# Three bf16 feature terms, 16-bit weights and running counts in PSUM in the ranked pass of a four-layer graph network

## The chip, the cores and the metric

The kernel runs on one core of a Trainium2 chip. The metric is device time in microseconds (us), the median over several executions. The engines of a core are named as the profile names them: PE (TensorE, matrix products; PEld is its weight load), DVE (VectorE), ACT (ScalarE), POOL (GpSimd) and SP (SyncE, which here issues the loads of the large matrix). PE multiplies from SBUF into PSUM, the accumulator memory, which the kernel uses in units of one bank: 128 partitions by 512 f32 values. The other engines read sums from there.

## The reference

Four layers on a graph of N = 3327 nodes with D = 64 features and a dense 3327 x 3327 f32 matrix `adj` (about half a per cent of its entries are not zero). Each layer normalizes x, applies a relu, and adds a graph network's result to x:

```python
# layer 0: two gated cells, each with m = adj @ (x @ W)
gi = m @ wih.T + bih;  gh = x @ whh.T + bhh
r = sigmoid(i_r + h_r);  z = sigmoid(i_z + h_z)
n = tanh(i_n + r * h_n)
x = relu((1.0 - z) * n + z * x)

# layer 1: ranked weights
support = input @ weight
mask = (adj != 0)
rank = cumsum(mask, axis=1);  deg = rank[:, -1:]
k = minimum(deg, 100.0)
pos = rank - (deg - k)
w = mask * where(pos > 0, 0.5 ** (k - pos), 0.0)
out = w @ support + bias

# layer 2: w = adj * adj; three times x = (w @ x) @ W.T + b
# layer 3: two times x = tanh(concat([adj @ x, x]) @ W[k])
```

That is eight passes over the matrix: two with adj, one with the ranked weights of layer 1, three with the squares, two with adj again. In the ranked weights an entry that is not zero counts the entries of its row that lie behind it, n of them, and weighs 0.5 to the power n if n is below 100.

## The kernel before

**Layout.** The nodes are padded to 26 blocks of 128, in two halves `s` of 13 blocks. The features of both halves stand side by side, so that a product with 128 weight columns comes as two instructions of 64 (`for h in range(2)`), one for each half. The nodes are cut into four chunks `CH` of 3, 3, 3 and 4 blocks: a chunk's sum is 384, 384, 384 or 512 columns wide. Chunks 0 and 1 are group 0, chunks 2 and 3 group 1 (`GROUPS`).

**Tiles of the matrix.** A tile is one block row of `adjT` (a source block `q`, 128 partitions) by the columns of one group in both halves, 768 or 896 KB. SP loads it into one of 19 slots `adj0` to `adj18` (L248). 286 loads are made. The list `units` holds the whole work in order as (pass, chunk, tile). `alone(g, k, order, sweep)` puts one pass for one group, tile by tile with both chunks of each, but for the last `sweep` tiles, which all go through chunk a first and then through chunk b, so that chunk a's sum is complete early. `joint` lets a tile serve two passes. The stages in order are: pass 0 of group 0, passes 0 and 1 of group 1, pass 1 of group 0, then pass 2 (the ranked pass) of group 0 and of group 1 with the source blocks in descending order and `sweep=0`, pass 3 of group 1, and four more (L584 to L594).

**One unit.** `run()` (L392) goes through the units. It prepares tiles 8 or 16 units ahead (`prepare`: load, and in the ranked pass the mask, L286, and the running count, L291), expands two units ahead (`expand`) and multiplies (`propagate`, L335): the chunk's sum in PSUM gains y of the source block times the tile's columns. On PE the ranked pass thus reads: counts of unit i+2, product of unit i, counts of unit i+3, and so on.

**Ranked weights.** `expand` counts in PSUM for each entry the entries behind it. The bf16 matrix `tri` counts inside a block (and subtracts 128 on the diagonal, which tells where the entry itself is not zero); `ones` times the running count of the blocks behind (`before.after`) adds the rest. Both go into a tile `ps` with two banks, one for each half s. L316 then makes 0.5 to the power n from that count on ACT: it scales by -2^23, adds a bias, clips at zero and writes the result as an int32 whose bits are read as an f32. The running count is the sum over all blocks before (L291, on DVE), in bf16, and lies with the mask in one slot (`Counts`). The product L335 takes y in f32, and 2^27 is worked into it beforehand (L452).

**PSUM.** Eight banks are drawn from two pools: four tiles `acc` of one bank each for the chunks' sums, and two tiles `ps` of two banks each, which all other products use (L310 in `expand`, `temps()` and `temp()` elsewhere).

**After a sum.** When a chunk has met its 26 source blocks, `propagate` starts that chunk's task, a generator `after_k`. It first copies the sum to SBUF (`evacuate`, L410 on DVE for even chunks, L408 on ACT for odd ones), then makes dense products and the normalization. `spend()` takes the time of each unit (`STREAM_US`) off every task's remaining delay and lets the task go on when that is used up, so the `yield` values set at which place among the products a task's instructions stand. `gru` (L465) makes the gated cell of layer 0: products for r and z into one tile `prz`, for n into another tile `pn` (L470), two sigmoids (L478, L479), two operations that read `pn` (L483, L484), tanh and the rest. `residual` (L457) adds to x from PSUM. `add_row` (L462, POOL) adds a bias. `after_1` normalizes with the factor 2^27 for the ranked pass and ends with `y[2][c] = yk`; the product of the ranked pass that needs this y finishes that task first.

The order of the instructions on every engine is the order in which this program emits them; nothing is moved later.

Of the kernel before, what the change touches and what calls it, by code (L numbers as in the profile page):

```python
# [11 lines left out]
I32 = mybir.dt.int32  # L12
# [26 lines left out]
N, D = 3327, 64  # L39
# [11 lines left out]
TWO23 = float(2 ** 23)  # L51
# [29 lines left out]
def kernel(  # L81
# [14 lines left out]
    psum = ctx.enter_context(tc.tile_pool(name="psum", bufs=4, space=bass.MemoryType.PSUM))  # L96
# [25 lines left out]
    ones = const.tile([P, P], BF16, name="ones")  # L122
# [4 lines left out]
    def more_constants():  # L127
        for h in range(2):
            hs = slice(h * D, (h + 1) * D)
            nc.vector.tensor_copy(bd[hs, :, hs], packed[hs])  # L130
        nc.gpsimd.memset(ones, 1.0)

        nc.gpsimd.affine_select(out=tri, in_=ones, pattern=[[-1, P]], compare_op=ALU.is_gt, fill=0.0,
                                base=0, channel_multiplier=1)
        nc.gpsimd.affine_select(out=tri, in_=tri, pattern=[[-1, P]], compare_op=ALU.not_equal, fill=-128.0,
                                base=0, channel_multiplier=1)
        nc.gpsimd.memset(bitsb, (CAP - 128.0) * TWO23)
        wide = work.tile([P, P], F32, name="t2")
        nc.gpsimd.memset(wide, 0.0)

        for i, (bi, bh) in enumerate(((BI1, BH1), (BI2, BH2))):
            nc.vector.tensor_add(bsum[:, i], bcol[:, bi:bi + 2], bcol[:, bh:bh + 2])

        nc.vector.tensor_scalar(wide[0:D], wide[0:D], bcol[0:D, BL1:BL1 + 1], None, op0=ALU.add)
        yield 3.0
        ps = temp()
        mm(ps[:, :D], wide, ident[:, :D])
        nc.vector.tensor_copy(brow[:, 3], ps[:, :D])

        for wt, ih in ((W1, IH1), (W2, IH2)):  # L150
            yield 1.0
            ps = temp()
            mm(ps[:, :P], bd[:, wt, :], ident)
            tr = work.tile([P, P], F32, name="t2")
            nc.scalar.copy(tr, ps[:, :P])
            yield 1.0
            ps = temp()
            mm(ps[:, :3 * P], tr, bd[:, ih:ih + 3, :].rearrange("p g f -> p (g f)"))
            nc.vector.tensor_copy(bd[:, ih:ih + 3, :].rearrange("p g f -> p (g f)"), ps[:, :3 * P])

# [4 lines left out]
    def width(c):  # L165
        return blocks(c) * P

    def mm(out, lhsT, rhs, start=True, stop=True):


        for h in range(2):
            hs = slice(h * D, (h + 1) * D)
            nc.tensor.matmul(out[hs], lhsT[:, hs], rhs, start=start, stop=stop)  # L173

    def temps():
        return psum.tile([P, 2, CWM], F32, name="ps", bufs=2)

    def temp():
        return temps()[:, 0]
# [21 lines left out]
    tasks = {}  # L201

    def advance(c):
        try:
            tasks[c][1] = next(tasks[c][0])
        except StopIteration:
            del tasks[c]

# [9 lines left out]
    def spend(us):  # L218

        for c in list(tasks):  # L220
            tasks[c][1] -= us
            if tasks[c][1] <= 0:
                advance(c)
# [8 lines left out]
    class Tile:  # L232

        def __init__(self, q, g, in_place):
            self.q, self.g, self.in_place, self.uses = q, g, in_place, 0
            self.b0 = CH[GROUPS[g][0]][0]
            self.w = sum(width(c) for c in GROUPS[g])
            self.slot = self.counts = self.before = None
            self.squares = set()
# [20 lines left out]
    class Counts:  # L260


        def __init__(self, w):
            self.slot = dead.popleft()
            both = slots[self.slot].bitcast(BF16).rearrange("p s w -> p (s w)")
            self.mask, self.after = (
                both[:, i * 2 * GWM:i * 2 * GWM + 2 * w].rearrange("p (s w) -> p s w", s=2) for i in range(2))

        def free(self):
            dead.append(self.slot)  # L270
# [9 lines left out]
    def prepare(k, c, t):  # L280

        if t.slot is None:
            t.load()
        if KIND[k] == RANKED and t.counts is None:
            t.counts, t.before = Counts(t.w), newest.get(t.g)
            nc.vector.tensor_scalar(t.counts.mask, t.view(), 0.0, None, op0=ALU.not_equal)  # L286
            t.used()
            if t.before is None:
                t.counts.after = t.counts.mask
            elif t.q > 0:  # L290
                nc.vector.tensor_tensor(t.counts.after, t.before.after, t.counts.mask, ALU.add)  # L291
            newest[t.g] = t.counts
        if KIND[k] == SQUARED and t.in_place and c not in t.squares:
            t.squares.add(c)
            square(t.view(c), t.view(c), t.q + c)

    def expand(k, c, t):

        w = width(c)
        if KIND[k] == PLAIN or t.in_place:  # L300
            return t.view(c)
        wide = work.tile([P, 2, CWM], F32, name="w4", bufs=4)[:, :, :w]
        if KIND[k] == SQUARED:
            square(wide, t.view(c), t.q + c)
            return wide

        ps = temps()  # L310
        for s in range(2):
            mm(ps[:, s, :w], tri, t.counts.mask[:, s, t.cols(c)], stop=t.before is None)
            if t.before is not None:
                mm(ps[:, s, :w], ones, t.before.after[:, s, t.cols(c)], start=False)
        spend(STREAM_US * w / CWM)
        nc.scalar.activation(wide.bitcast(I32), ps[:, :, :w], AF.Relu, bias=bitsb, scale=-TWO23)  # L316
        if c == GROUPS[t.g][1]:
            if t.before is not None:
                t.before.free()
            if t.q == 0:  # L320
                t.counts.free()
        return wide

    def propagate(k, c, t, rhs, first, last):
        w = width(c)
        s, b = divmod(t.q, NB)
        cs = chunk_of(b)
        if y[k][cs] is None:
            finish(cs)
        if first:  # L330
            sums[k, c] = psum.tile([P, CWM], F32, name="acc")
        acc = sums[k, c]
        yq = y[k][cs][:, b - CH[cs][0], s, :]
        for h in range(2):
            nc.tensor.matmul(acc[h * D:(h + 1) * D, :w], yq, rhs[:, h, :], start=first, stop=last)  # L335
        if KIND[k] != RANKED:
            t.used()
        spend(STREAM_US * w / CWM)
        if last:
            begin(c, after[k](c, sums.pop((k, c))))  # L340

# [63 lines left out]
    def evacuate(acc, c):  # L405
        m = work.tile([P, CWM], F32, name="t2")[:, :width(c)]
        if c % 2:
            nc.scalar.copy(m, acc[:, :width(c)])  # L408
        else:
            nc.vector.tensor_copy(m, acc[:, :width(c)])  # L410
        return m

    def dense_to_nodes(terms, c):

        v = view(temp(), c)
# [4 lines left out]
        return v  # L420

    def transpose_to_nodes(ft, c):
        v = view(temp(), c)
        for b in range(blocks(c)):
            mm(v[:, b, :], ft[:, b * P:(b + 1) * P], ident)
        return v

    def transpose_to_features(h, c):
        ps = temp()
# [3 lines left out]
        nc.scalar.copy(ft, ps[:, :width(c)])  # L433
        return ft
# [21 lines left out]
    def residual(v, c):  # L456
        nc.vector.tensor_tensor(flat(xchunk(c)), flat(xchunk(c)), v, ALU.add)  # L457
# [7 lines left out]
    def gru(acc, c, hT, ih, hh, bi, bh, cell):  # L465
# [4 lines left out]
        prz, pn = temps(), temps()  # L470
        for g in range(2):
            mm(prz[:, g, :w], bd[:, hh + g, :], hT, stop=False)
            mm(prz[:, g, :w], bd[:, ih + g, :], m, start=False)
        for g, (wt, ft) in enumerate(((hh + 2, hT), (ih + 2, m))):
            mm(pn[:, g, :w], bd[:, wt, :], ft)
        rz = work.tile([P, 2, CWM], F32, name="w4", bufs=4)
        r, z = rz[:, 0, :w], rz[:, 1, :w]
        nc.scalar.activation(r, prz[:, 0, :w], AF.Sigmoid, bias=bsum[:, cell, 0:1])  # L478
        nc.scalar.activation(z, prz[:, 1, :w], AF.Sigmoid, bias=bsum[:, cell, 1:2])  # L479
# [3 lines left out]
        nc.vector.scalar_tensor_tensor(t, pn[:, 0, :w], bcol[:, bh + 2:bh + 3], r, op0=ALU.add, op1=ALU.mult)  # L483
        nc.vector.tensor_tensor(t, t, pn[:, 1, :w], ALU.add)  # L484
# [8 lines left out]
        return o  # L493

# [9 lines left out]
    def after_0(c, acc):  # L504
        hT[c] = yield from gru(acc, c, hT[c], IH1, HH1, BI1, BH1, 0)
        v = transpose_to_nodes(hT[c], c)
        yield 0.8
        yk = nodes(c)
        nc.vector.tensor_copy(flat(yk), v)
        y[1][c] = yk  # L510

    def after_1(c, acc):
# [7 lines left out]
        y[2][c] = yk  # L520
# [12 lines left out]
    def after_hop(k):  # L533
        def done(c, acc):
# [6 lines left out]
            nc.vector.tensor_tensor(groups(yk), v.rearrange("p b (s d) -> p (b s) d", d=D),  # L541
                                    brow[:, k - 3:k - 2, :].to_broadcast([P, n, D]), ALU.add)
            y[k + 1][c] = yk
# [14 lines left out]
    def after_6(c, acc):  # L558
# [4 lines left out]
        nc.scalar.activation(flat(yk), v, AF.Tanh)  # L563
# [4 lines left out]
    def after_7(c, acc):  # L568
# [4 lines left out]
        nc.scalar.activation(flat(t), v, AF.Tanh)  # L573
        yield 0.8
        residual(flat(t), c)
# [68 lines left out]
```

## Time and profile before

The profile is of one execution; its time lies 0.55 us above the median of the runs.

| | us |
|---|---|
| median of 9 runs (lowest, highest) | 769.35 (768.61, 769.9) |
| the profiled execution's own time | 769.9 |
| its span in the profile | 766.9 |
| ranked products, sum of 104 units (L335 from `w`, with the squares not made in place) | 128.2 busy |
| ranked counts (L173, `tri` and `ones`) | 72.9 + 70.8 busy |
| running counts on DVE (L291), 48 times | 50.6 busy |
| masks on DVE (L286), 52 times | 53.8 busy |
| weights on ACT (L316), 104 times | 99.3 busy |

A row of a group reads: line, engine, operation, output from inputs, shape and type, how often; then busy time and the mean in ns of one; then the idle time of the engine just before these instructions, and what ended most of it. Consecutive matmuls overlap in the records, so a matmul's own duration is longer than the step from one start to the next. A row of a timeline reads: start, duration, engine, line, operation, output from inputs, shape, number; in brackets the engine's idle time before it and what ended it. The idle time before the copies L410 is DVE's, not PE's.

### The profile page before, as it was taken

The page shows a single profiled execution, that of the slowest core. Times are in us where ns is not written, and L with a number is a line of the kernel's source. Part 1 is how long each engine was busy: PE and PEld are TensorE (multiplying, and loading weights), DVE is VectorE, ACT ScalarE, POOL GpSimd, SP SyncE. Part 2 cuts the span into 40 slices and gives each one's busy share as a digit, 9 for nine tenths or more (in the row PEclk, how much of TensorE's full clock was granted, in tenths as well). Part 3 has the DMA queues.
Part 4 walks back from the last instruction along what each step waited for, and adds up shares of the span by engine and source line. Part 5 has one row for each costly group of instructions (what it writes and reads, how often), then busy time and mean ns, then how long its engine had stood idle before and what let it go on. Part 6 is the DMA issues. An engine that isn't in the chain of part 4 may idle for free.

```text
span 766.9 us, 11891 instructions
## 1 busy us (share of the span) xinstructions
PE 735.0 (96%) x5032; PEld 349.4 (46%) x5032; DVE 278.4 (36%) x386; ACT 247.1 (32%) x306; POOL 44.4 (6%) x37
## 2 busy tenths in 40 slices
PE   3978999999989999999999999999999999999997
PEld 2423433444545555556434444434344445344444
DVE  6102101226779958970774121513062520000000
ACT  1101001011046676666985431733034601000000
POOL 5000000002003001200200000000020010000000
PEclk9999999999999999999999999999999999999999
DMA  9999994789977998999999948990998389915991
GB/s 290 401 401 406 406 406 172 274 320 403 401 268 253 331 355 290 314 359 406 406 402 400 401 191 320 405 404 15 352 391 294 136 304 405 379 59 196 401 402 73
DMA packets 79172, 245.25 MB, mean 320 GB/s; under 512 B 4880, under 2 KB 5520, under 8 KB 79120
## 3 DMA queue, kind: packets, MB, share of 16 engines
q1 hardware_dynamic: 78240, 243.55, 84.5%
q10 hardware_dynamic: 880, 0.96, 0.5%
q8 instruction: 39, 0.64, 0.3%
q14 instruction: 13, 0.11, 0.0%
HBM read 243.64 MB, written 0.85 MB: 319 GB/s over the span
## 4 chain that ended last, share of the span: by engine, by line
PE 83%; DMA 8%; DVE 6%; SPq 1%; ACT 1%; issue 1%; POOL 0%; ACTq 0%; DVEq 0%; POOLq 0%
PE acc L335 67%; PE ps L173 16%; DMA adj<-in_adjT 7%; SPq L248 1%; DMA brow<-in_bias_rows 1%; DVE adj L291 1%; DVE adj L286 1%; ACT w L316 1%; DVE xs L457 0%; DVE st L447 0%; DVE st L441 0%; DVE w L276 0%; DVE t L446 0%; DVE t L443 0%; DVE w L483 0%
## 5 line engine op out<-in xcount | busy, mean ns | idle before, releaser
L335 PE MATMUL acc<-adj,y 128*64 128x384 f32 (+1 forms) x2704 | 489.6, 516 | 20.9 <-DMA adj<-in_adjT 20.5
L335 PEld LDWEIGHTS acc<-adj,y 128*64 128x64 f32 x2704 | 194.3, 137 | 286.4 <-issue 235.0
L335 PE MATMUL acc<-w,y 128*64 128x384 f32 (+1 forms) x624 | 128.2, 504 | 1.7 <-DVE w L276 0.8
L410 DVE COPY t<-acc 128x384 f32<-128x384 f32 x16 | 8.9, 558 | 294.4 <-PE acc L335 294.4
L316 ACT ACTIVATE w<-ps,bitsb 128x768 int32<-128x768 f32 x104 | 99.3, 956 | 48.8 <-PE ps L173 45.6
L274 ACT ACTIVATE adj<-adj 128x768 f32<-128x768 f32 (+1 forms) x103 | 86.3, 906 | 29.2 <-DMA adj<-in_adjT 29.2
L173 PE MATMUL ps<-adj,tri 128*64 128x384 bf16 (+1 forms) x416 | 72.9, 339 | 2.2 <-DVE w L484 1.4
L173 PE MATMUL ps<-adj,ones 128*64 128x384 bf16 (+1 forms) x400 | 70.8, 339 | 0.0
L276 DVE TENSOR_TENSOR adj<-adj 128x768 f32<-128x768 f32 (+1 forms) x53 | 53.8, 1064 | 46.1 <-DMA adj<-in_adjT 46.1
L449 POOL TENSOR_TENSOR st<-st,mhalf 128x6 f32<-128x6 f32 (+1 forms) x16 | 28.4, 1772 | 575.4 <-DVE st L448 575.4
L335 PEld LDWEIGHTS acc<-w,y 128*64 128x64 f32 x624 | 47.0, 137 | 27.4 <-issue 14.3
L286 DVE TENSOR_SCALAR adj<-adj 128x1536 bf16<-128x1536 f32 (+1 forms) x52 | 53.8, 1037 | 9.0 <-DMA adj<-in_adjT 9.0
L478 ACT ACTIVATE w<-ps,bsum 128x384 f32<-128x384 f32 (+1 forms) x8 | 4.9, 609 | 154.7 <-PE ps L173 154.7
L291 DVE TENSOR_TENSOR adj<-adj,adj 128x1536 bf16<-128x1536 bf16 (+1 forms) x48 | 50.6, 1054 | 2.9
L173 PEld LDWEIGHTS <-tri 128*64 128x64 bf16 x416 | 28.0, 110 | 29.1 <-issue 22.9
L173 PEld LDWEIGHTS <-ones 128*64 128x64 bf16 x400 | 26.4, 110 | 24.5 <-issue 20.0
L274 ACT ACTIVATE w<-adj 128x768 f32<-128x768 f32 x35 | 27.6, 839 | 15.9 <-PE acc L335 9.5
L408 ACT COPY t<-acc 128x384 f32<-128x384 f32 (+1 forms) x16 | 8.5, 532 | 70.1 <-PE acc L335 70.1
L173 PE MATMUL ps<-bd,t 128*64 128x128 f32 (+1 forms) x320 | 26.1, 279 | 0.7 <-ACT t L408 0.4
L433 ACT COPY hT<-ps 128x384 f32<-128x384 f32 (+1 forms) x12 | 6.1, 507 | 63.4 <-PE ps L173 63.4
L276 DVE TENSOR_TENSOR w<-adj 128x768 f32<-128x768 f32 x17 | 16.0, 957 | 26.3 <-PE acc L335 19.8
L173 PEld LDWEIGHTS ps<-bd,t 128*64 128x64 f32 x320 | 19.1, 137 | 9.4 <-issue 4.2
(58 smaller groups left out, 248.9 us busy)
## 6 DMA issues: line engine op xcount, KB each, us to landing
adj<-in_adjT SPq DMA_DIRECT2D x156, 768.0 KB, 9.9
adj<-in_adjT SPq DMA_DIRECT2D x130, 896.0 KB, 10.4
adj<-in_weights SPq DMA_DIRECT2D x2, 352.0 KB, 7.8
xs<-in_x SPq DMA_DIRECT2D x1, 640.0 KB, 4.8
out<-xs ACTq DMA_DIRECT2D x3, 192.0 KB, 1.9
out<-xs ACTq DMA_DIRECT2D x1, 256.0 KB, 6.3
xs<-in_x SPq DMA_DIRECT2D x1, 192.0 KB, 2.5
brow<-in_bias_rows ACTq DMA_DIRECT2D x1, 96.0 KB, 7.5
```

What stands on the lines that cost most here:

```text
L173: nc.tensor.matmul(out[hs], lhsT[:, hs], rhs, start=start, stop=stop)
L248: nc.sync.dma_start(out=slots[self.slot][:, :, :self.w], in_=adjT[self.q * P:(self.q + 1) * P, :].rearrange("p (s w) -> p s w", s=2)[:, :, ...
L274: nc.scalar.activation(sq, v, AF.Square)
L276: nc.vector.tensor_tensor(sq, v, v, ALU.mult)
L286: nc.vector.tensor_scalar(t.counts.mask, t.view(), 0.0, None, op0=ALU.not_equal)
L291: nc.vector.tensor_tensor(t.counts.after, t.before.after, t.counts.mask, ALU.add)
L316: nc.scalar.activation(wide.bitcast(I32), ps[:, :, :w], AF.Relu, bias=bitsb, scale=-TWO23)
L335: nc.tensor.matmul(acc[h * D:(h + 1) * D, :w], yq, rhs[:, h, :], start=first, stop=last)
L408: nc.scalar.copy(m, acc[:, :width(c)])
L410: nc.vector.tensor_copy(m, acc[:, :width(c)])
L433: nc.scalar.copy(ft, ps[:, :width(c)])
L449: nc.gpsimd.tensor_tensor(st[:, 3, :n], st[:, 2, :n], mhalf[:, :n], ALU.pow)
```

## The change

The ranked pass is rebuilt, and with it the way in which PSUM is shared out.

- **Products.** `in_three` splits a chunk's y into three bf16 parts (copy to bf16, subtract, twice), which lie in a slot of the matrix. In the ranked pass `propagate` multiplies three times, once for each part, all with bf16 weights. `expand` writes the weights as 16-bit exponents (scale -2^7, int16, read as bf16).
- **Counts.** The running count is no longer made on DVE (L291 goes). It stays in PSUM: the count of a chunk lies in a pair of banks through its 26 tiles. For each tile PE adds `rest` (`ones` less `tri`) times the mask of the block behind and `tri` times the mask of the block itself, ACT reads the sum, and PE goes on adding. A mask takes half a slot (`Mask`).
- **PSUM.** Four tiles of two banks each, `bank0` to `bank3`, are allocated once. Sums are drawn from the first four banks (`take(sums=True)`), other products from the last four, singly; they are returned with `give`. While counts are kept, the last four banks hold them and the other products draw from the first four too. `gru` takes a bank for each of r, z and the two halves of n, and each sigmoid stands right behind its own products.

```diff
+    pairs = [psum.tile([P, 2, CWM], F32, name=f"bank{i}") for i in range(4)]
+    idle_sums, idle_temps = deque(range(4)), deque(range(4, 8))
+    counting = []
+
+    def bank(i):
+        return pairs[i // 2][:, i % 2]
+
+    def take(sums=False):
+        pool = idle_sums if sums or counting else idle_temps
+        for c in list(tasks):
+            if not pool and c not in running:
+                advance(c)
+        i = pool.popleft()
+        return i, bank(i)
+
+    def give(i):
+        (idle_sums if i < 4 else idle_temps).append(i)
...
-            if t.before is None:
-                t.counts.after = t.counts.mask
-            elif t.q > 0:
-                nc.vector.tensor_tensor(t.counts.after, t.before.after, t.counts.mask, ALU.add)
...
-        ps = temps()
+        if not counting:
+            while len(idle_temps) < 4:
+                advance(next(iter(tasks)))
+            counting.append(True)
+        a, b = GROUPS[t.g]
+        pair = pairs[2 if c == a else 3]
         for s in range(2):
-            mm(ps[:, s, :w], tri, t.counts.mask[:, s, t.cols(c)], stop=t.before is None)
             if t.before is not None:
-                mm(ps[:, s, :w], ones, t.before.after[:, s, t.cols(c)], start=False)
+                mm(pair[:, s, :w], rest, t.before.view[:, s, t.cols(c)], start=False, unchecked=True)
+            mm(pair[:, s, :w], tri, t.mask.view[:, s, t.cols(c)], start=t.before is None, unchecked=True)
-        nc.scalar.activation(wide.bitcast(I32), ps[:, :, :w], AF.Relu, bias=bitsb, scale=-TWO23)
+        nc.scalar.activation(wide, pair[:, :, :w], AF.Relu, bias=bitsb, scale=-TWO7)
...
         if first:
-            sums[k, c] = psum.tile([P, CWM], F32, name="acc")
+            sums[k, c] = take(sums=True)
...
+        terms = y[k][cs] if KIND[k] == RANKED else [y[k][cs]]
+        for n, yk in enumerate(terms):
+            yq = yk[:, b - CH[cs][0], s, :]
+            for h in range(2):
+                nc.tensor.matmul(acc[h * D:(h + 1) * D, :w], yq, rhs[:, h, :], start=first and n == 0,
+                                 stop=last and n == len(terms) - 1)
...
-        spend(STREAM_US * w / CWM)
+        spend(STREAM_US * w / CWM * (0.75 if KIND[k] == RANKED else 1.0))
...
-        prz, pn = temps(), temps()
-        for g in range(2):
-            mm(prz[:, g, :w], bd[:, hh + g, :], hT, stop=False)
-            mm(prz[:, g, :w], bd[:, ih + g, :], m, start=False)
-        for g, (wt, ft) in enumerate(((hh + 2, hT), (ih + 2, m))):
-            mm(pn[:, g, :w], bd[:, wt, :], ft)
+        for g, gate in enumerate((r, z)):
+            i, ps = take()
+            mm(ps[:, :w], bd[:, hh + g, :], hT, stop=False)
+            mm(ps[:, :w], bd[:, ih + g, :], m, start=False)
+            nc.scalar.activation(gate, ps[:, :w], AF.Sigmoid, bias=bsum[:, cell, g:g + 1])
+            give(i)
+        pn = take(), take()
+        for (_, ps), wt, ft in zip(pn, (hh + 2, ih + 2), (hT, m)):
+            mm(ps[:, :w], bd[:, wt, :], ft)
...
+    def in_three(h, c):
+        g = c // 2
+        if g not in parts:
+            parts[g] = dead.popleft()
+        n = blocks(c) * 2 * D
+        first = 3 * 2 * D * blocks(GROUPS[g][0]) if c == GROUPS[g][1] else 0
+        room = slots[parts[g]].bitcast(BF16).rearrange("p s w -> p (s w)")
+        terms = [room[:, first + i * n:first + (i + 1) * n] for i in range(3)]
+        hf = h.rearrange("p b s d -> p (b s d)")
+        for i in range(2):
+            yield 0.8
+            nc.scalar.copy(terms[i], hf)
+            yield 0.8
+            nc.vector.tensor_tensor(terms[2] if i else hf, hf, terms[i], ALU.subtract)
+        return [t.rearrange("p (b s d) -> p b s d", s=2, d=D) for t in terms]
...
-        y[2][c] = yk
+        y[2][c] = yield from in_three(yk, c)
```

The lines of the changed kernel that the prediction speaks of have new numbers: the copy of a sum on DVE is L454 (L410 before), the sigmoids are L525, gru's reads of n L533 and L534, the ranked read of the counts L353, the product L376.

## The prediction

> **What bounds the kernel now.** I read the page first: the busy times, then the chain that ended last, then the costliest groups.
>
> ```profile
> PE 735.0 (96%) x5032; PEld 349.4 (46%) x5032; DVE 278.4 (36%) x386; ACT 247.1 (32%) x306; POOL 44.4 (6%) x37
> ...
> L335 PE MATMUL acc<-w,y 128*64 128x384 f32 (+1 forms) x624 | 128.2, 504 | 1.7 <-DVE w L276 0.8
> L410 DVE COPY t<-acc 128x384 f32<-128x384 f32 x16 | 8.9, 558 | 294.4 <-PE acc L335 294.4
> L316 ACT ACTIVATE w<-ps,bitsb 128x768 int32<-128x768 f32 x104 | 99.3, 956 | 48.8 <-PE ps L173 45.6
> L173 PE MATMUL ps<-adj,tri 128*64 128x384 bf16 (+1 forms) x416 | 72.9, 339 | 2.2 <-DVE w L484 1.4
> ...
> L291 DVE TENSOR_TENSOR adj<-adj,adj 128x1536 bf16<-128x1536 bf16 (+1 forms) x48 | 50.6, 1054 | 2.9
> ```
>
> PE is busy 735.0 of 766.9 us, and 67% of the chain are products (L335), 16% products into temporaries (L173). Of what the change touches, only PE's own work pays directly. Next, the waits and the stages (columns: stretch, length, busy time and count of each engine, clock, DMA share, GB/s):
>
> ```profile
> PE acc L335 <- DMA adj<-in_adjT: 20.5, 15, 13.1
> ```
>
> ```profile
> 62.00:123.00 61.00, 60.17 (x348) 24.64 (x350) 8.46 (x16) 3.71 (x7) 0.00 (x0) 1.00 1.00 395
> ...
> 212.00:244.00 32.00, 27.65 (x244) 16.77 (x242) 26.42 (x44) 16.87 (x22) 6.46 (x4) 1.00 0.74 260
> 244.00:288.00 44.00, 44.00 (x410) 25.60 (x408) 32.94 (x34) 30.70 (x35) 0.00 (x0) 1.00 0.95 331
> 288.00:355.00 67.00, 66.27 (x542) 39.59 (x540) 49.56 (x56) 44.37 (x45) 7.68 (x4) 1.00 0.93 333
> ```
>
> The timeline puts PE's last wait for a load at 62.83. After that PE is full but for the ranked pass's start (212 to 244, 4.35 us idle). The clock is 1.00 throughout. The timeline gives the prices: two steady units of the ranked pass, an evacuation, and the last stall of the start.
>
> ```profile
> 254.41 0.33 PE L173 MATMUL ps<-adj,tri 128*64 128x384 bf16 x2
> 254.57 0.33 PE L173 MATMUL ps<-adj,ones 128*64 128x384 bf16 x2
> 254.74 0.33 PE L173 MATMUL ps<-adj,tri 128*64 128x384 bf16 x2
> 254.90 0.33 PE L173 MATMUL ps<-adj,ones 128*64 128x384 bf16 x2
> 255.06 0.81 PE L335 MATMUL acc<-w,y 128*64 128x384 f32 x4
> 255.71 0.33 PE L173 MATMUL ps<-adj,tri 128*64 128x384 bf16 x2
> ```
>
> ```profile
> 63.52 0.14 PEld L335 LDWEIGHTS acc<-adj,y 128*64 128x64 f32 x2 [0.18 <-issue]
> 63.74 0.56 DVE L410 COPY t<-acc 128x384 f32<-128x384 f32 x1 [33.83 <-PE acc L335]
> ```
>
> ```profile
> 242.06 0.87 PE L335 MATMUL acc<-w,y 128*64 128x384 f32 x4 [0.69 <-DVE y L453]
> ```
>
> Starts, not durations, give PE's rate, since matmuls overlap: a bf16 pair (one per half of the channels) takes 0.161 us at 384 columns, an f32 product 0.645 (255.06 to 255.71), four times as much. The 512-wide rows give 0.215 and 0.86.
>
> **Ranked products, the gain.** 104 units become three bf16 pairs: 78 of 384 columns save 0.645 − 3×0.161 = 0.161 each, 26 of 512 save 0.215: 12.6 + 5.6 = 18.15 us. The counts keep four bf16 pairs per unit, so they cost the same. Of the 18.15, the first 15 units (2.4 us) lie in the start of the pass, treated below; 89 units remain: **−15.7**. The reads of the counts by ACT (L316) stay 104; a 16-bit instead of 32-bit output I bound between the same 0.90 and 1.12 us of today and half of that. At 2.02 us in a tile of now 2.63 (g = 1) ACT still has room: 0.
>
> **What becomes cheaper off the path.** 48 running adds (L291, 50.6 us of DVE) go; masks take half slots. DVE is 36% busy and no row has PE waiting for L291: 0 outside the start. Splitting y into three terms adds two ACT copies and two DVE subtractions per chunk (nearest rows: 0.53 and 0.55), 2.2 us of work each; chunks 2 and 3 are first used just as the pass starts, chunks 0 and 1 later. Cover gone, a chunk would cost its 2.2.
>
> **Loads.** Tiles stay longer ahead in slots. Before, loads land every 1.96 to 2.26 us where DMA is saturated (338 to 452) and PE does not wait for any; the loads after the pass keep some 8 us of lead, so a pass that ends 16 us earlier would still be fed. I take 0; at worst the first tiles of the next stage come 2 us late.
>
> **The waits that the change adds.** PE's order outside the ranked pass is the same. But the four tiles of PSUM are now `pairs`, each with two banks, and in the built program a write waits for readers of the whole tile. Before, each sum was a tile of its own: at 63.52 PE loads weights for the next chunk's sum while L410 copies the first from 63.74 to 64.30. Afterwards both sums of a group are halves of one pair, and the first product of chunk b, right behind the last of chunk a with no work between, waits for the copy. This is so at 15 places, at a 16th with 0.43 us of work between. The price: the copy starts 0.21 after PE's next issue, takes 0.56, and PE restarts 0.06 after a DVE end (L453 ends at 242.00, PE starts at 242.06): 0.83, plus 0.05 that the first group after a wait takes longer (0.70 against 0.645) = **0.89**. What is queued behind it is all of PE.
>
> In gru() the same happens with z: before, r and z were a pair and pn another. Now pn's first product shares its pair with z, and waits for z's sigmoid: 0.22 to 0.28 until ACT starts, 0.57, 0.06, 0.05 = 0.935 (1.04 at 512, where the sigmoid takes 0.68). 8 places. Upside in the same function: r's sigmoid no longer waits for z's products, 1.29 earlier; PE does not wait on that outside the start.
>
> 13 of the evacuations lie outside the ranked pass's two ends: 13 × 0.89 = **+11.6**. Six gru places: 4 × 0.935 + 2 × 1.04 = **+5.8**. The Trainium skill's page "PSUM — Partial Sum Buffer", section "PSUM bank collisions raise a hardware error", asks that engines be kept apart by bank and quadrant, no further. By that rule the two halves, different banks, need no wait; the trace of before agrees (the row at 63.74), but the built program's waits go by the tile. By the rule the 17.4 us of the last two terms would be gone and the time about 752.6; by the program's waits it is the sum below.
>
> **The start of the ranked pass.** Before, PE idles 4.36 us there in six gaps, and the last one ends with y for chunk 1 at 242.00. Afterwards PE would have less work (2.4) and none of these stalls (with 0.2 each for modelled ends, 5.6), but one evacuation (0.89), two sigmoid waits (1.87), and the first sums, which take banks that were just temporaries: unit 1 waits for a residual add (about 0.9) and unit 2 for gru's sum (about 1.45). That puts PE in front of the first product with chunk 1's y at about 239.2. It then waits for the three terms: the normalized y ends near 238.1 (3.9 earlier: r's head start of 1.29, and two or three adds of 0.96 to 1.64 gone from DVE's queue in front of it), and copy, subtraction, copy, subtraction follow, each 0.55 plus 0.25 to 0.5 behind L316 on ACT (0.90) or a mask on DVE (0.95): 241.2 to 242.4 against 242.0 before. So DVE and ACT set this moment, not PE: **−0.3**, between −0.8 and +0.4; what was saved in front of it is lost.
>
> **The end of the pass and the seam.** The last two units' savings wait behind ACT, and chunk 3's first copy is met by the last evacuation: +0.5 to +1.0, taken **+0.75**. At the seam between the two column groups the 16th wait costs 0.89 − 0.43 = 0.46; against it stand PE's two gaps there before (0.32 at 289.97, 0.41 at 295.57, about 0.5 each with their modelled ends), of which I let 0.9 go, since the counts of the new group are ready earlier: **−0.44**. Existing gaps of PE next to new waits (141.18, 562.84, 612.32, about 0.5 each with their modelled ends) are absorbed: **−1.5**.
>
> **Sum:** −15.7 − 0.3 + 0.75 + 11.6 + 5.8 − 0.44 − 1.5 = +0.2. On the profiled execution (766.9 span + 3.0 around it = 769.9) that is 770.1; it lies 0.55 above the median of the runs, so the sum for the median is about 769.6. The waits are the side on which rows are above my price, so I round up: **770.0**. A measurement of this kernel tells 0.2% (1.5 us) from no change: the forecast is no measurable change.
>
> **Rivals.**
> - *The waits cost more than a bare copy* (slower, one mechanism: the restart of PE at each of the 23 places). One evacuation before ran 1.01 us after PE's issue because DVE was busy; one restart took 0.24 longer (PE at 180.46, 1.10 for 0.86 of work). With 0.11 to 0.24 more at 23 places: +2.5 to +5.5, 772 to 775. It decides from about 0.05 per place (770.9). For it: the 1.01 and 1.10 rows. Against: 14 of 16 copies at the same 0.83. Chance 0.36.
> - *The start gains more, or waits overlap* (faster): the three terms arrive early enough, PE goes through at 239.2, −2.8 instead of −0.3, or a third of the evacuations hide behind work: 764 to 767.8. For it: DVE loses 50 us of adds. Against: four handoffs between ACT and DVE. Chance 0.20.
> - *The waits do not bind*: the whole 18 counts and some stalls go: 752 to 756. It needs PE to have other work at 23 places, and the order of the program has none. Chance 0.06.
> - *The gain is given back to DMA*: PE waits for no load after 62.83 and keeps 8 us of lead, so I give this nothing of its own; a full give-back would be +15.7, 785.7, which those 8 us speak against. That ACT becomes the bound of the pass is excluded by 2.02 in 2.63.
>
> **Numbers.** No measurable change 0.38 (its own range 767.8 to 770.9), slower 0.36, faster 0.26 (0.20 + 0.06). The range 765 to 775 leaves out the far case and the tails of the others, together about 0.2.
>
> **What would show it.** Steady tiles of the pass 2.26 instead of 2.59 (g = 0) and 2.63 instead of 3.02 (g = 1); no L291; a wait of PE's sums for the evacuating DVE copy, about 15 × 0.9, and of PE's temporaries for a sigmoid, 8 × 0.9, which no view of before has; no wait of PE for DMA after 63 us. If those waits are missing or short, the time falls to the fast cases; if PE waits for loads between 355 and 420, my lead is wrong.

## The result, and the profile after

The changed kernel takes 772.27 us in the median (10 runs, 770.69 to 774.38), the kernel before 769.21 (31 runs, 768.21 to 770.35): a ratio of 1.0042, with a 95% interval of 1.0034 to 1.0050. It is slower by 3.1 us, a little more than a measurement of this kernel can tell from no change. The time lies within the predicted range, 2.3 us above the predicted 770.0, and on the side of the first rival. The profiled execution took 771.27 with a span of 769.5 (before: 769.9 and 766.9). The executions of one kernel differ with the granted clock that each shows (of the changed kernel's, six at 0.999 or 1.0, the profiled one among them, took 770.69 to 771.66, four at 0.997 or 0.998 took 772.88 to 774.38, and one at 0.999 took 773.31), so where medians and profiled executions differ the text gives both. The 2.6 us between the two spans, taken apart below, are a little less than the 3.1 of the medians.

First the page of the changed kernel: busy times, and the groups that answer to those shown of before.

```profile
PE 721.0 (94%) x5240; PEld 356.9 (46%) x5240; DVE 235.9 (31%) x346; ACT 251.4 (33%) x314; POOL 42.0 (5%) x38
...
L353 ACT ACTIVATE w<-bank,bitsb 128x768 int16<-128x768 f32 x104 | 99.0, 955 | 31.0 <-PE bank L179 30.2
...
L454 DVE COPY t<-bank 128x384 f32<-128x384 f32 x16 | 8.9, 558 | 280.7 <-PE bank L376 280.7
L376 PE MATMUL bank<-w,adj 128*64 128x384 bf16 (+1 forms) x624 | 73.9, 340 | 4.5 <-ACT adj L561 1.4
```

PE is busy 14 us less than before and yet ends 2.6 us later: its work has become waiting. The row of the ranked products is now bf16 (before they stood with the squares in a row of 128.2 us). The 16-bit output changed nothing for ACT: 955 ns an operation against 956. The waits (engine, line and what it waited for; total, times, longest) show the two kinds that before did not have at all, 14 and 8 times, where the prediction counted 15 and 8:

```profile
PE bank L376 <- DMA adj<-in_adjT: 19.0, 15, 12.0
...
PE bank L376 <- DVE t L454: 10.7, 14, 1.9
...
PE bank L179 <- ACT w L525: 5.7, 8, 0.8
```

The stages, in the columns explained in the prediction:

```profile
62.00:123.00 61.00, 58.83 (x336) 23.51 (x338) 8.09 (x15) 3.93 (x7) 0.00 (x0) 1.00 0.99 391
212.00:244.00 32.00, 26.80 (x254) 16.00 (x256) 21.35 (x39) 14.94 (x21) 2.54 (x2) 1.00 1.02 392
244.00:288.00 44.00, 42.32 (x520) 29.28 (x518) 22.36 (x26) 34.23 (x41) 2.99 (x2) 1.00 0.98 373
288.00:355.00 67.00, 66.78 (x724) 49.23 (x722) 30.89 (x39) 51.00 (x53) 5.70 (x4) 1.00 0.93 352
```

From 62 to 123 us, far from the ranked pass, PE loses 1.3 us of busy time. In the pass it is as full as before, with 724 instead of 542 instructions from 288 to 355. The timeline of the changed kernel shows both waits, and the steady pass:

```profile
63.06 0.56 DVE L454 COPY t<-bank 128x384 f32<-128x384 f32 x1 [33.36 <-PE bank L376]
63.67 0.20 PEld L376 LDWEIGHTS bank<-adj,y 128*64 128x64 f32 x4 [1.33 <-DVE t L454]
63.67 1.51 PE L376 MATMUL bank<-adj,y 128*64 128x384 f32 x8 [0.66 <-DVE t L454]
```

```profile
217.29 0.58 ACT L525 ACTIVATE w<-bank,bsum 128x384 f32<-128x384 f32 x1 [0.65 <-PE bank L179]
...
217.93 0.87 PE L179 MATMUL bank<-hT,bd 128*64 128x384 f32 x4 [0.68 <-ACT w L525]
```

```profile
251.74 0.65 PE L376 MATMUL bank<-w,adj 128*64 128x384 bf16 x6
...
254.02 0.65 PE L376 MATMUL bank<-w,adj 128*64 128x384 bf16 x6
```

At the start of the ranked pass the same wait is longer. There DVE comes to the copy only after a mask (L320) that waited for its load, and PE stands idle for 1.93 us:

```profile
211.67 0.96 DVE L320 TENSOR_SCALAR adj<-adj 128x1536 bf16<-128x1536 f32 x1 [0.97 <-DMA adj<-in_adjT]
212.55 0.55 DVE L454 COPY t<-bank 128x384 f32<-128x384 f32 x1
...
213.16 1.51 PE L376 MATMUL bank<-adj,y 128*64 128x384 f32 x8 [1.93 <-DVE t L454]
```

At the first two places the copy ends at 63.62 and PE starts at 63.67; the sigmoid ends at 217.87 and PE starts at 217.93. Two units of group 0 take 2.28 us (251.74 to 254.02), 2.26 was predicted and 2.59 is the row of before.

Because the order of the 832 units is the same in both kernels, the start of each unit's product can be set against the same unit's start before. The difference jumps where time is lost or won:

| where (time in the changed kernel) | jump of PE's lateness, us |
|---|---|
| 13 evacuations outside the ranked pass | 0.83 (9 times), 0.85, 0.90, 0.90, 0.92: +11.0 |
| 6 waits for z's sigmoid (69.8 to 181.2) | 0.90, 0.90, 0.95, 1.01, 0.95, 1.07: +5.8 |
| an old gap that vanishes (145.5) | −0.5 |
| start of the ranked pass (213.2 to 251.7) | +2.1 at the evacuation, +1.2 in all |
| the pass from there to its last units | −15.6, of it −0.6 at the seam |
| its last two units | +0.3 |
| a product of the next stage that waits for a square on DVE (378.95) | +0.7 |

With −0.7 in the first 60 us, where loads set the time and the runs differ from each other by as much as 0.9, and 0.4 spread over the units between, these make the 2.6 us by which the span grew.

### The profile page after: what moved, and what is told of

Its sections match the earlier page's. It is cut to its first block, busy times and chain, and to the rows that moved or that the text cites. A ratio compares the mean times of both kernels' runs of the same rounds, so it can differ in the third digit from the quotient of the medians.

```text
span 769.5 us, 12248 instructions
## 1 busy us (share of the span) xinstructions
PE 721.0 (94%) x5240; PEld 356.9 (46%) x5240; DVE 235.9 (31%) x346; ACT 251.4 (33%) x314; POOL 42.0 (5%) x38
## 4 chain that ended last, share of the span: by engine, by line
PE 79%; DMA 10%; DVE 6%; ACT 1%; SPq 1%; issue 1%; POOL 1%; ACTq 0%; DVEq 0%; POOLq 0%
PE bank L376 63%; PE bank L179 16%; DMA adj<-in_adjT 9%; SPq L273 1%; DVE t L454 1%; DMA brow<-in_bias_rows 1%; POOL st L497 1%; ACT w L525 1%; DVE st L489 0%; DVE st L495 0%; DVE xs L505 0%; DVE t L494 0%; ACT w L353 0%; DVE y L501 0%; DVE t L491 0%
## 5 line engine op out<-in xcount | busy, mean ns | idle before, releaser
L376 PE MATMUL bank<-adj,y 128*64 128x384 f32 (+1 forms) x2704 | 492.5, 517 | 29.8 <-DMA adj<-in_adjT 19.0
L376 PEld LDWEIGHTS bank<-adj,y 128*64 128x64 f32 x2704 | 197.4, 137 | 294.8 <-issue 212.4
L353 ACT ACTIVATE w<-bank,bitsb 128x768 int16<-128x768 f32 x104 | 99.0, 955 | 31.0 <-PE bank L179 30.2
L454 DVE COPY t<-bank 128x384 f32<-128x384 f32 x16 | 8.9, 558 | 280.7 <-PE bank L376 280.7
L376 PE MATMUL bank<-w,adj 128*64 128x384 bf16 (+1 forms) x624 | 73.9, 340 | 4.5 <-ACT adj L561 1.4
L179 PE MATMUL bank<-adj,tri 128*64 128x384 bf16 (+1 forms) x416 | 72.4, 339 | 0.0
L179 PE MATMUL bank<-adj,rest 128*64 128x384 bf16 (+1 forms) x400 | 70.3, 339 | 0.0
L320 DVE TENSOR_SCALAR adj<-adj 128x1536 bf16<-128x1536 f32 (+1 forms) x52 | 53.1, 1027 | 49.9 <-PE bank L179 40.3
L525 ACT ACTIVATE w<-bank,bsum 128x384 f32<-128x384 f32 (+1 forms) x16 | 9.7, 609 | 139.5 <-PE bank L179 139.5
L376 PEld LDWEIGHTS <-adj 128*64 128x64 bf16 x624 | 40.0, 110 | 20.4 <-issue 2.3
L376 PE MATMUL bank<-w,y 128*64 128x384 f32 x208 | 36.6, 488 | 1.5 <-DVE w L310 0.8
L179 PEld LDWEIGHTS <-rest 128*64 128x64 bf16 x400 | 25.7, 110 | 9.9 <-issue 0.5
L179 PE MATMUL bank<-bd,t 128*64 128x128 f32 (+1 forms) x320 | 26.0, 279 | 0.6 <-ACT t L452 0.4
```

The source lines that it names most:

```text
L320: nc.vector.tensor_scalar(t.mask.view, t.view(), 0.0, None, op0=ALU.not_equal)
L353: nc.scalar.activation(wide, pair[:, :, :w], AF.Relu, bias=bitsb, scale=-TWO7)
L454: nc.vector.tensor_copy(m, acc[1][:, :width(c)])
L525: nc.scalar.activation(gate, ps[:, :w], AF.Sigmoid, bias=bsum[:, cell, g:g + 1])
```

## The experiments

Time before was measured beside each: 769.11 for the first four, 769.12 for the next four, 768.97 and 769.22 for the last. All ratios are to it.

**Take the sums apart (e1).** The first question was whether the waits for the copies are the loss, or whether PE would wait there anyway.

```diff
-    pairs = [psum.tile([P, 2, CWM], F32, name=f"bank{i}") for i in range(4)]
+    singles = [psum.tile([P, CWM], F32, name=f"sum{i}") for i in range(4)]
+    pairs = [None, None] + [psum.tile([P, 2, CWM], F32, name=f"bank{i}") for i in (2, 3)]
...
-        return pairs[i // 2][:, i % 2]
+        return singles[i] if i < 4 else pairs[i // 2][:, i % 2]
```

> The changed kernel, but the four banks for the chunks' sums are four tiles of one bank each instead of two tiles of two; nothing else differs. Theory T (the changed kernel loses at each evacuation because PE's first product into one half of a pair waits for the copy out of the other half): the shifts of PE at the 15 places add up to 13.7 us in the trace of the changed kernel, so about 758.6 (757 to 761), and PE no longer waits for the DVE copy. Rival R1 (the waits only stand where PE would have waited anyway, for loads or other engines, so that the gain is given back): 769 or more, with new waits for DMA. Rival R2 (the three bf16 products gained less than their rows say, and the waits are short): 769 to 772.

757.35 us, ratio 0.9848 (0.9832 to 0.9864): 14.9 us below the changed kernel in the median, and 13.7 by the spans of the profiled executions (755.8 against 769.5), as expected. The timeline of e1 at the first place (L455 is the copy, `sum` the single banks):

```profile
62.21 2.16 PE L377 MATMUL sum<-adj,y 128*64 128x384 f32 x12 [1.11 <-DMA adj<-in_adjT]
...
63.12 0.56 DVE L455 COPY t<-sum 128x384 f32<-128x384 f32 x1 [33.70 <-PE sum L377]
```

PE's twelve products from 62.21 on run through the copy without a break, the copy takes the same 0.56, and no row has a wait of PE's products for L455. Theory T holds; R1 and R2 fall: no wait for loads came in its place.

**Hand the temporaries out in turn (e2), and both (e3).** e2 keeps the shared pairs of sums and changes one line; e3 has both edits.

```diff
-    idle_sums, idle_temps = deque(range(4)), deque(range(4, 8))
+    idle_sums, idle_temps = deque(range(4)), deque((4, 6, 5, 7))
```

> The changed kernel, but the four temporary banks are handed out in the order 4, 6, 5, 7, so that two banks taken one after the other lie in different pairs; the sums stay in shared pairs. T: 7 of the 8 places in gru lose the wait of PE for z's sigmoid (0.90 to 1.07 each); the second product for n then stands 0.645 behind and waits some 0.2: 7 x 0.95 - 6 x 0.2 = 5.5 us less, 766.8 (766 to 768). R1 and R2: 771 to 773.

> Both edits together: sums in four tiles of their own, temporaries in the order 4, 6, 5, 7. T: 772.3 - 13.7 - 5.5 = 753.1 (751 to 756), clearly faster than the kernel before. R1: with the ranked pass and the stages behind it some 20 us earlier, PE meets the loads: waits for DMA after 63 us of 10 us or more, 763 or more. R2: 766 or more.

e2 takes 770.08, ratio 1.0008 (0.9997 to 1.0020), 2.2 us less than the changed kernel in the median and not 5.5. By the spans of the profiled executions it is 3.5 us less (766.0 against 769.5). e3 takes 753.24, ratio 0.9803 (0.9787 to 0.9818), as expected and 15.9 us faster than the kernel before. In e2 the six places before the ranked pass gain 0.65, 0.65, 0.65, 0.86, 0.64 and 0.92 by the units' starts, 4.4 us in all, but 1.7 us are lost again at one place: the evacuation at the start of the pass, where PE's wait for the copy grows from 1.93 to 3.67. The timeline of e3 shows what stands there, now as a wait of gru's product that needs the copy:

```profile
204.49 0.96 DVE L321 TENSOR_SCALAR adj<-adj 128x1536 bf16<-128x1536 f32 x1 [1.03 <-DMA adj<-in_adjT]
...
206.40 0.96 DVE L321 TENSOR_SCALAR adj<-adj 128x1536 bf16<-128x1536 f32 x1 [0.95 <-DMA adj<-in_adjT]
207.27 0.55 DVE L455 COPY t<-sum 128x384 f32<-128x384 f32 x1
...
207.88 0.87 PE L179 MATMUL bank<-t,bd 128*64 128x384 f32 x4 [1.91 <-DVE t L455]
```

The sum was complete near 204, but DVE runs its queue in order, and two masks (L321) in front of the copy each wait for a tile of the matrix to arrive. However early PE comes, the loads decide when the copy ends. This is theory Q of the later runs.

**Put the pairs into the kernel before (e4).** The same cost, added where nothing else is changed:

```diff
+    sum_pairs = [psum.tile([P, 2, CWM], F32, name=f"acc{i}", bufs=1) for i in range(2)]
+    idle_sums = deque(range(4))
...
-            sums[k, c] = psum.tile([P, CWM], F32, name="acc")
-        acc = sums[k, c]
+            sums[k, c] = idle_sums.popleft()
+        i = sums[k, c]
+        acc = sum_pairs[i // 2][:, i % 2]
```

> The kernel before, with the one edit that the four banks of the chunks' sums are the halves of two tiles; the ranked pass is as before. T: 15 places x 0.85 = 12.7 us more, 782 (780 to 783), with PE waiting for the copy on DVE 15 times. R1: stalls move but the time stays, 769 to 771. R2: up to 773.

785.24, ratio 1.0215 (1.0197 to 1.0232): 16.1 us more, with the row

```profile
PE acc L339 <- DVE t L414: 12.1, 15, 2.6
```

Thirteen places cost 0.83 to 0.92 by the units' starts, as in the changed kernel, and one at the end of the ranked pass 0.5. The one at the start of the pass cost 2.8, since the copy stands behind masks and running adds there, and 1.6 more came right behind it. That 1.6 is no wait: for 3.41 us the granted clock fell to 0.50 (the column behind POOL), and PE's work took twice as long.

```profile
209.13:212.54 3.41, 3.41 (x14) 1.30 (x12) 3.30 (x4) 0.00 (x0) 0.00 (x0) 0.50 1.00 341
```

So the mechanism is settled from both sides; the expectation was 3 us too low by that one place and by the clock.

**Undo the three terms (e5).** e3, with the f32 product, the 32-bit weights and the tasks' pace of before; counts in PSUM stay. The lines that matter most:

```diff
-        terms = y[k][cs] if KIND[k] == RANKED else [y[k][cs]]
+        terms = [y[k][cs]]
...
-        y[2][c] = yield from in_three(yk, c)
+        y[2][c] = yk
```

> The kernel of e3 (sums in four tiles, temporaries alternating), but the ranked pass multiplies one f32 y by 32-bit weights as before, without the split into three terms; counts still stay in PSUM and DVE still makes no running adds. Theory T: the products lose their 18.15 us, the split's wait of PE at the start (1.43 + 0.24) goes, its DVE and ACT work too: 753.2 + 18.2 - 1.7 = 769.7 (768 to 771.5), so the counts in PSUM and the new handing out of banks are worth nothing by themselves. Rival: the three terms gain less than 18 (their 312 pairs of weight loads show): below 766; or the counts in PSUM gain by themselves: below 766 as well, told apart by the length of a steady tile, 2.59 if the products cost what their rows say.

765.54, ratio 0.9952 (0.9937 to 0.9967). The products' price is right: from one unit's product to the next it takes 1.295 us (252.43, 253.73, 255.02), 2.59 for two, and e5 loses 15.0 us to e3 between the start of the pass and its end. But it is 4.2 us faster than expected. Against the kernel before it wins 3.3 us by the units' starts, 2.5 of them between 220 and 293 us and 0.6 at the seam: what is left of the change without the three terms does gain by itself, most of it in the start of the pass (rival). Which part of it gains (no running adds on DVE, masks in half slots, gru's earlier sigmoid for r) no run separates. And e3, with the three terms, loses 2.2 us to e5 up to the end of that start, although its products there are shorter.

**Is DVE's time off the path (e6)?** e3, with each mask written twice, which gives DVE back about the time of the running adds.

```diff
             nc.vector.tensor_scalar(t.mask.view, t.view(), 0.0, None, op0=ALU.not_equal)
+            nc.vector.tensor_scalar(t.mask.view, t.view(), 0.0, None, op0=ALU.not_equal)
```

> The kernel of e3 with each mask written twice: 52 more operations of about 1.03 us on DVE, as much as the running adds took (48 x 1.054). It asks whether that time on DVE was off the path. By the prediction's 0: 753.2 within 1 us. Rival Q (a copy out of PSUM or a normalization that stands behind masks in DVE's queue is late by them): at the start of the ranked pass DVE is busy 26.5 of 35 us, so some 1 us later for each mask in front of a link of the chain for chunk 1's y: 754.5 to 757.

761.99, ratio 0.9905 (0.9888 to 0.9922): 8.75 us more than e3 in the median, 7.3 by the spans of the profiled executions (759.0 against 751.7), and more than rival Q gave. All of it (7.4 by the units' starts) is lost before 252 us; behind that, nothing. In DVE's timeline of e6 (L321 and L322 are the two masks) the normalization of chunk 1's y (L502, L503) stands in line:

```profile
240.89 1.76 DVE L321 TENSOR_SCALAR adj<-adj 128x1536 bf16<-128x1536 f32 x1
242.68 0.96 DVE L322 TENSOR_SCALAR adj<-adj 128x1536 bf16<-128x1536 f32 x1
243.56 0.16 DVE L502 TENSOR_SCALAR st<-st 128x6 f32<-128x6 f32 x1
243.75 0.56 DVE L503 SCALAR_TENSOR_TENSOR y<-t,st 128x384 f32<-128x384 f32 x1
```

Not all of the 7.4 is DVE's time. Twice in this stretch, from 230.81 and from 247.88 us, the granted clock fell to 0.50 for 3.41 us, both times behind a wait of PE of 1.98 us:

```profile
247.88:251.29 3.41, 3.41 (x22) 1.98 (x24) 3.34 (x4) 0.90 (x1) 0.00 (x0) 0.50 0.72 236
```

Work that takes twice as long for 3.41 us loses 1.7, so the clock explains up to 3.4 of the 7.4 and the masks in DVE's queue at least 4.0 (an estimate from these rows). In e3 DVE is 31% busy over the span and free in the steady pass, but in the start of the pass more work on it makes the kernel longer.

**Copy on ACT (e7), and the split without pauses (e8).** e7 is e3 with the late copy moved to ACT, whose queue is free there; e8 sets the split's delays to 0 as well.

```diff
-        if c % 2:
+        if c % 2 or on_act:
```

> The kernel of e3, but chunk 0's sum of the pass before the ranked one is copied out by ACT, not DVE, where the copy stood behind a mask that waited for its load; PE waited 1.91 for it. Theory Q: the wait goes, and everything behind it moves up: 751.3 (750.8 to 752). Rival: the loads set the pace here (masks wait for DMA in front of the ranked pass), so that PE finds the next wait later: 753 unchanged.

> e7, and the four steps of the split into three terms are emitted with no pause between them (delays 0.8 become 0), so that they stand earlier in the queues of ACT and DVE. In e3 PE waits 1.43 + 0.24 for them. Expected 0.5 to 1.5 less than e7: 750.3 (749.5 to 751). Rival: the chain's start (normalization) sets it, or an earlier step only blocks ACT's reads of the counts behind it: as e7 or up to 1 more.

753.14, ratio 0.9794 (0.9777 to 0.9810), and 753.39, ratio 0.9794 (0.9780 to 0.9809): no gain over e3's 753.24. In e7 PE comes to gru's products 2.1 us earlier and loses 1.75 of it two units on, where it waits 1.58 us for gru's sum on DVE, which stands in the same queue behind the same masks. The rival holds: moving one reader only shows the next. In e8 the split's steps come earlier in the queues, and nothing is gained.

**A slot less (e9).** Why are the masks later than in e5? The three terms of chunks 2 and 3 take a slot of the matrix already before the pass. e9 is e5 with the slots taken and nothing put in.

```diff
+        if c // 2 not in parts:
+            parts[c // 2] = dead.popleft()
         y[2][c] = yk
```

> The kernel of e5 (f32 products, no split), but the two slots that would hold the three terms are taken out of the rotation at the end of the same tasks and given back at the same place, with nothing written to them. Theory S (the split makes the start of the ranked pass late also because a slot less is left for loads, so that loads, masks and the copy of the sum behind a mask come one tile later): masks ahead of the pass about 2 us later than in e5, PE waits for the copy some 1.9 as in e3, and 766 to 767.5. Rival: the loads are late in e3 for another reason (the pacing of tasks), 765.5 as e5 and masks at the same times.

767.14, ratio 0.9977 (0.9967 to 0.9987): 1.6 more than e5, and the copy starts at 206.91 against 204.92, one tile later. PE's new wait for it is 1.07, less than the expected 1.9, since in this trace PE is 0.9 us later already from the loads of the first 60 us; the rest of S holds.

**Masks later in DVE's queue (e10, e11).** e3, with a mask emitted 12 (e10) or 8 (e11) units ahead and the loads as before.

```diff
+            while masked < min(prepared, i + 12):
+                prepare_mask(*units[masked])
+                masked += 1
```

> The kernel of e3, but a tile's mask is emitted 12 units ahead, not with its load 16 units ahead; loads as before. Theory Q2 (the copy of a sum, the reads of gru and the normalization are late because they stand in DVE's queue behind masks that wait for loads): two masks fewer stand in front of the copy, the 1.91 us wait goes and the chain for chunk 1's y moves up: 751 to 752.5. Rival: later masks free slots later, loads come later, and the pass waits for masks: 753 to 756.

> As e10, with masks 8 units ahead. Q2: no mask waits for a load any more in front of the copy; the start of the pass gains up to the whole 1.9 + 1.7 us of PE's waits there: 749.5 to 752. Rival: slots come free later, loads fall behind: 754 or more, with PE or DVE waiting for DMA in the pass.

751.12, ratio 0.9768 (0.9753 to 0.9782), and 751.24, ratio 0.9769 (0.9752 to 0.9785). In the timeline of e10 the copy (L463) now waits for PE, and the mask stands behind it:

```profile
203.93 0.56 DVE L463 COPY t<-sum 128x384 f32<-128x384 f32 x1 [1.10 <-PE sum L381]
204.41 0.95 DVE L323 TENSOR_SCALAR adj<-adj 128x1536 bf16<-128x1536 f32 x1
```

PE is 2.1 us earlier from there to the end; 8 units give no more than 12, since what is left in the start (1.43 + 0.24 for the terms) does not come from masks that wait for loads (the last is an inference; no run takes it apart). e10 is the fastest kernel of the study, 17.9 us faster than the kernel before.

**The same edit in the changed kernel (e12).**

> The changed kernel itself, pairs and all, with the one edit of e10: masks 12 units ahead, not 16. Theory Q2 (in the changed kernel the evacuation at the start of the ranked pass cost 2.12 us, not 0.89, because the copy stood behind a mask that waited for its load): the wait at that place falls to 0.66 in the record, as at the 14 others, and PE stays 1.2 us or more earlier from there on: 770 to 771.2 against 772.3. Rival (the loads hold PE there whatever DVE's order): 772 to 773, and the wait shows up at the next reader.

770.29, ratio 1.0011 (1.0002 to 1.0020), 2.0 below the changed kernel in the median and 1.2 by the spans (768.3 against 769.5). The evacuation at the start waits 0.65 instead of 1.93 in the record, PE is 1.2 us earlier from there on and nothing else moves. Q2 holds for the step that the prediction missed.

## Why the prediction was right or wrong

- **The gain of the products** (−15.7 for 89 units, −0.44 at the seam): measured −15.0, as e5 gives, and −0.6 at the seam, where the gap at 295.57 is gone. Right in mechanism and nearly in size.
- **The 13 evacuations** (0.89 each, +11.6): 0.83 to 0.92, +11.0. **The six sigmoids** (+5.8): +5.8. That a write waits for readers of the other half was shown both ways: without it −14.9 (e1), with it in the kernel before +16.1 (e4, 1.6 of it the clock).
- **The rule of the Trainium skill** ("PSUM — Partial Sum Buffer", section "PSUM bank collisions raise a hardware error"), by which halves in different banks need no wait, put the time at about 752.6. In e3, where nearly all of these waits are gone, PE writes one bank while DVE copies another in the same 0.56 us, and the time is 753.24. Rule and runs agree; the wait was the program's, not the chip's. That the two times lie so close is partly luck: by the spans e3 is 15.2 below the kernel before, where the sum without the two terms says 17.2.
- **The start of the pass** (−0.3, between −0.8 and +0.4): +1.2, outside the bounds. The term that failed is "one evacuation (0.89)": it cost 2.1, since the copy stood in DVE's queue behind a mask that waited for its load; with the mask later in the queue 0.8 is left (e12). The place was in front of me in the trace of before, where the copy runs behind a running add:

```profile
203.93 0.17 PEld L335 LDWEIGHTS acc<-adj,y 128*64 128x64 f32 x2
204.46 0.96 DVE L291 TENSOR_TENSOR adj<-adj,adj 128x1536 bf16<-128x1536 bf16 x1
205.34 0.55 DVE L410 COPY t<-acc 128x384 f32<-128x384 f32 x1
```

From the weight load of the next chunk's first product (203.93) to the copy's start it is 1.41 us, not the 1.01 of the prediction and not the 0.21 of the price. That DVE is busy there was read rightly; that the adds would go and the waits of the masks for their loads stay was not followed up. The expected wait for the three terms is there (1.44 + 0.24).

- **The absorbed gaps** (−1.5): only the one at 141.18 went, −0.5. The one at 562.84 was 0.23 in the record, less than the prediction put it at, and is still 0.14; the one at 612.32 is there as before (0.33): it waits for a square and lies several units behind the new waits, not beside them.
- **The end of the pass** (+0.75): +0.3. The last evacuation of the pass adds no wait of its own: PE waits there for the weights from ACT (0.95 at 362.32).
- **A wait without a term**: at 378.95 PE waits 0.74 for a square that stands in DVE's queue behind the normalizations of chunks 2 and 3. It is there without the shared pairs too (0.73 in e3).
- **L291 off the path** ("0 outside the start"): true in the steady pass; in the start e6 prices 53 us of DVE's time at 4 us or more, and e5 shows a gain of about 3 without the adds, of which they may be a part only. In e3 most of that gain is spent on the later copy and the split (2.2 against e5).
- **Loads** (0, at worst 2 us late in the next stage): PE waits for no load, but a slot less made the masks one tile later in front of the pass; that costs 1.6 us in e9 (medians).

So the sum was +0.2 and the trace has +2.6: 1.5 from the start, 1.0 from gaps not absorbed, 0.7 from the square, less 0.5 for the evacuations; the first 60 us (−0.7) and what is spread (+0.4) nearly cancel, and the pass with its seam and its end comes out as priced. The forecast of no measurable change was a small loss instead. The time lies in the range because the range was wide enough for the first rival. That rival of dearer waits came nearest in time, but not by its mechanism: PE's restart costs what was priced at every place but one, and that one was dearer by the load in front of it.

## What to carry to other kernels

Buffers that are read by one engine while another fills their neighbour belong in tiles of their own: here four banks as two tiles of two cost 0.83 to 0.92 us of PE at each of 13 places and 2.1 at a 14th, and with the same wait in gru they undid a real gain of some 16 us. When time is taken off the busiest engine, look for new waits in stages that the change does not concern, by setting the start of the same unit in both traces side by side. And in an engine that runs its queue in order, put what waits for a load behind what another engine is waiting for: moving the masks four units back was worth 2.1 us in e3, while moving the copy to another engine gained nothing.

## What was not expected of the hardware

DVE's share of busy time said little: 31% over the span, yet 53 us of needless work on it cost 7.3 us by the spans, all within 50 us of one stage.

Part of that is the clock. Between 20 us and the last 5 us the granted clock is 1.00 in every profiled execution but two: it fell to 0.50 for 3.41 us once in e4, behind a wait of PE of 2.58 us, and twice in e6, behind waits of 1.98. Each time PE's work took twice as long (a step of two bf16 products 0.32 us, not 0.16). A wait of 1.93 us in the changed kernel and one of 3.67 in e2 left the clock at 1.00, so these traces show no length of a wait that brings it on.
